# Pair products with batch norm: rows of a pair matrix stored from two permanent slots, a long row beside a short one

## The chip, the core and the metric

The kernel runs on one core of a Trainium2 chip. A core has five engines that work beside each other: TensorE (PE in the profile), VectorE (DVE), ScalarE (ACT), GpSimd (POOL) and SyncE (SP), which here only issues transfers. Data come from HBM into SBUF (128 partitions) and go back by 16 DMA engines. The metric is the device time of one execution in microseconds (us); the median of three runs before the change is 2237.81 us (2237.63 to 2238.28).

## The reference

```python
B, F0, F1, E, C = (256, 39, 39, 16, 1)        # the inputs have 1024 samples
_ROWS, _COLS = np.tril_indices(F1, k=-1)      # 741 pairs (r, c) with c < r
cross = xj[:, rows, :, None] * xi[:, cols, None, :]
mean = jnp.mean(cross, axis=(0, 2, 3), keepdims=True)
var = jnp.mean(jnp.square(cross - mean), axis=(0, 2, 3), keepdims=True)
normed = (cross - mean) * jax.lax.rsqrt(var + BN_EPS)
normed = normed * gamma[None, :, None, None] + beta[None, :, None, None]
out = normed[:, :, None, :, :] * W[None, None, :, :, :]
return jnp.transpose(out, (0, 2, 1, 3, 4))
```

For each of 1024 samples and 741 pairs (r, c) the 16 x 16 outer product of row r of `xj` and row c of `xi` is normalised with the pair's mean and variance over all samples and multiplied by `W`. All is float32. The inputs are 2.6 MB each; the output, 1024 x 741 x 256 numbers, is 777 MB.

## The kernel before, in words

**Layout.** Each of the 128 partitions holds 8 samples (`NT` = 8). A pair of one sample is 256 numbers, 1 KB; this is called a unit here. In the output the pairs of a row r lie side by side, so that r pairs of one sample are one run of r KB.

**Statistics.** The first part of the kernel computes, for each pair, a scale s and a shift t from sums over the samples; they end in `st_sb`, two numbers for each of the 741 pairs, the same on every partition. The last step of it (lines 216 to 234) goes through groups of rows, `ROW_GROUPS`: VectorE spreads a group on a diagonal (L219), TensorE multiplies it with ones (L226), and ScalarE copies each row of the group from PSUM to its place in `st_sb` (L234, 38 copies in all). Then ScalarE copies `W` into PSUM for VectorE (`w_dve`).

**Tiles.** The main part goes through tiles. A tile is one row r (all r pairs with c < r) for `nt` of a partition's 8 samples. `samples(r)` takes the largest of 1, 2, 4, 8 with nt x r at most `UNITS` = 76: eight samples up to row 9, four for rows 10 to 19, two from row 20 on. The order of rows is 6, 7, ..., 38, then 5, 4, ..., 1; that makes 105 tiles. The buffers `y` (up to 76 units) and `xs` have two copies each.

**The three steps of a tile k.**
- `scale_xi(k)` (L256, GpSimd): xs = s times `xi`, one instruction.
- `products(k)`: y = xs times one number of `xj`. Above row 6, for each sample and each i of 16, one instruction over r x 16 numbers: ScalarE does 12 values of i (L282), GpSimd 4 (L284). In rows 1 to 6 VectorE does a whole sample in one instruction (L272).
- `finish(k)`: (y + t) times W. Of the pairs above row 6 some 13% (from `split` on) are GpSimd's: one L313 for each pair, adding t, then one L317 for all of them, multiplying by W. The other pairs are VectorE's, one L297 each, over all nt samples. SyncE stores `16 // nt` pairs at a time as VectorE gets them done (runs of 2, 4 or 8 KB), and GpSimd's pairs in a store of their own at the end (L307).

**Order.** All is written out by hand under `manual_schedule`, and each engine works in the order of the program: finish(k), products(k+1), scale_xi(k+2). Waits between engines follow from what is read and written: products wait for xs and until the buffer's stores have landed, finish waits for the products, a store for its pairs. SyncE issues the stores in their order, and a store that has to wait holds up those behind it.

Of the kernel before, what the change touches and what calls it, by code (L numbers as in the profile page):

```python
# [7 lines left out]
F32 = mybir.dt.float32  # L8
AF = mybir.ActivationFunctionType
ALU = mybir.AluOpType  # L10
# [3 lines left out]

VECTOR_ROW = 6

UNITS = 76

POOL_I = 4
POOL_SHARE = 0.13  # L20

DEV_ON_VECTOR = ((2, 1), (4, 1), (6, 1))

ROW_GROUPS = ((1, 7), (7, 13), (13, 19), (19, 25), (25, 31), (31, 37), (37, 39))


@with_exitstack
def tile_pair_outer_batchnorm(
# [15 lines left out]
    nc = tc.nc  # L44
    P = nc.NUM_PARTITIONS
    NB, F, E = xi.shape
    NT = NB // P
    EE = E * E
# [4 lines left out]
    xi_sb = cpool.tile([P, NT, F, E], F32, name="xi_sb")  # L53
    xj_sb = cpool.tile([P, NT, F, E], F32, name="xj_sb")
    w_sb = cpool.tile([P, 1, EE], F32, name="w_sb")
    st_sb = cpool.tile([P, 2, NP], F32, name="st_sb")
    s_sb = st_sb[:, 0:1].unsqueeze(3)
    t_sb = st_sb[:, 1]
# [3 lines left out]
    out_v = out.rearrange("(p t) o n i j -> p t (o n i j)", t=NT)  # L62
# [6 lines left out]
    with tc.tile_pool(name="stat", bufs=1) as st, tc.tile_pool(  # L69
        name="dev", bufs=3  # L70
    ) as devp, tc.tile_pool(name="ps", bufs=1, space=bass.MemoryType.PSUM) as psp, tc.tile_pool(
        name="psx", bufs=3, space=bass.MemoryType.PSUM
# [6 lines left out]
        for r in range(1, F):  # L79
            n0 = first[r]  # L80
# [99 lines left out]
        u, v = shift_r, shift[0:F, 1, :]  # L180
        stt = nc.vector.scalar_tensor_tensor

        def small(name):
            return st.tile([F, F], F32, name=name)

        k, q1, q2, var, rstd, inv = (small(n) for n in ("k", "q1", "q2", "var", "rstd", "inv"))
# [28 lines left out]

        for r0, r1 in ROW_GROUPS:
            n = r1 - r0
# [19 lines left out]
    w_dve = wpsp.tile([P, 1, EE], F32, name="w_dve")  # L237
# [1 line left out]

    def samples(r):
        return max(n for n in (1, 2, 4, 8) if NT % n == 0 and (n == 1 or n * r <= UNITS))

    order = list(range(VECTOR_ROW, F)) + list(range(VECTOR_ROW - 1, 0, -1))
    tiles = [(r, t0, samples(r)) for r in order for t0 in range(0, NT, samples(r))]

    rows = ctx.enter_context(tc.tile_pool(name="rows", bufs=2))
    scaled = ctx.enter_context(tc.tile_pool(name="scaled", bufs=2))
    xs_of, y_of = {}, {}  # L250

    def scale_xi(k):
        r, t0, nt = tiles[k]
        n0 = first[r]
        xs = scaled.tile([P, nt, r, E], F32, tag="xs", name=f"xs_{r}_{t0}")
        nc.gpsimd.tensor_tensor(  # L256
            xs,
            xi_sb[:, t0 : t0 + nt, 0:r, :],
            s_sb[:, :, n0 : n0 + r, :].to_broadcast([P, nt, r, E]),
            ALU.mult,  # L260
        )
        xs_of[k] = xs

    def products(k):

        r, t0, nt = tiles[k]
        xs = xs_of.pop(k)
        y = rows.tile([P, nt, r, E, E], F32, tag="y", name=f"y_{r}_{t0}")
        y_of[k] = y
        for t in range(nt):  # L270
            if r <= VECTOR_ROW:
                nc.vector.tensor_tensor(  # L272
                    y[:, t],
                    xs[:, t].unsqueeze(2).to_broadcast([P, r, E, E]),
                    xj_sb[:, t0 + t, r : r + 1, :].unsqueeze(3).to_broadcast([P, r, E, E]),
                    ALU.mult,
                )
                continue
            for i in range(E):
                scale = xj_sb[:, t0 + t, r, i : i + 1]  # L280
                if i < E - POOL_I:
                    nc.scalar.activation(y[:, t, :, i, :], xs[:, t], AF.Copy, scale=scale)  # L282
                else:
                    nc.gpsimd.tensor_scalar(  # L284
                        y[:, t, :, i, :], xs[:, t], scale, 1.0, ALU.mult, ALU.mult
                    )

    def finish(k):

        r, t0, nt = tiles[k]  # L290
        n0 = first[r]
        y = y_of.pop(k).rearrange("p t n i j -> p t n (i j)")
        split = r - (int(r * POOL_SHARE + 0.5) if r > VECTOR_ROW else 0)
        step = max(1, 16 // nt)

        def pair(c):
            nc.vector.scalar_tensor_tensor(  # L297
                y[:, :, c, :],
                y[:, :, c, :],
                t_sb[:, n0 + c : n0 + c + 1],  # L300
                w_dve.to_broadcast([P, nt, EE]),
                ALU.add,
                ALU.mult,
            )

        def store(c0, c1):
            nc.sync.dma_start(  # L307
                out_v[:, t0 : t0 + nt, (n0 + c0) * EE : (n0 + c1) * EE],
                y[:, :, c0:c1, :].rearrange("p t n e -> p t (n e)"),
            )  # L310

        for c in range(split, r):
            nc.gpsimd.tensor_scalar(  # L313
                y[:, :, c, :], y[:, :, c, :], t_sb[:, n0 + c : n0 + c + 1], 1.0, ALU.add, ALU.mult
            )
        if split < r:
            nc.gpsimd.tensor_tensor(  # L317
                y[:, :, split:r, :],
                y[:, :, split:r, :],
                w_sb.unsqueeze(1).to_broadcast([P, nt, r - split, EE]),  # L320
                ALU.mult,
            )
        for c0 in range(0, split, step):
            c1 = min(c0 + step, split)
            for c in range(c0, c1):
                pair(c)
            store(c0, c1)
        if split < r:
            store(split, r)

    with tc.manual_schedule():
        scale_xi(0)
        products(0)
        scale_xi(1)
        for k in range(len(tiles)):
            finish(k)
            if k + 1 < len(tiles):
                products(k + 1)
            if k + 2 < len(tiles):
                scale_xi(k + 2)  # L340


# [26 lines left out]
```

## Time and profile before

| what | value |
|---|---|
| median of three runs | 2237.81 us |
| the profiled execution's own time | 2239.29 us |
| span of its trace | 2237.6 us |
| VectorE busy | 1758.6 us (79%) |
| ScalarE busy | 1523.6 us (68%) |
| GpSimd busy | 1428.4 us (64%) |
| TensorE busy | 18.7 us (1%) |
| stores' queue (q1), share of 16 engines | 86.8% |
| HBM written | 776.99 MB |
| mean rate over the span | 350 GB/s |

How to read the profile: the page gives each engine's busy time, then the span in 40 equal slices, where a digit is the busy share of a slice in tenths (9 is 90% or more) and the DMA row is the mean share of the 16 DMA engines. A stretch is the same for a time span that one chooses. A group is all instructions of one line and shape: busy time, the mean duration of one in ns, and after the bar the idle time of the engine ahead of them, with what ended it. A row in order of time gives start, duration, engine, line, and how many instructions it merges (x24); in brackets stands the idle time ahead of it and what ended it. "issue" means that the profile shows nothing that was waited for. L297 is line 297 of the kernel.

### The profile page before, as it was taken

To read this page: it belongs to the slowest core of one execution; us is meant where nothing else is said; L and a number is where in the kernel's file an instruction comes from. 1 tells how busy PE (TensorE), PEld (TensorE's weight loads), DVE (VectorE), ACT (ScalarE), POOL (GpSimd) and SP (SyncE) were. 2 spreads that over 40 slices of the span, in tenths; PEclk is the share of its full clock that TensorE was granted. 3 is DMA by queue.
4 is the path that set the end of the run, shared out by engine and by line. 5 is a ranking of instruction groups with operands and counts; after the bars stand their busy time and mean duration, and the time that the engine had idled before them with its cause. 6 is when DMAs were issued, how large, how long until landed. Compare 5 with 4: busy or idle time off the path is not lost. (4 is left out here: it accounts for less than half of the span.)

```text
span 2237.6 us, 9393 instructions
## 1 busy us (share of the span) xinstructions
PE 18.7 (1%) x70; PEld 11.9 (1%) x70; DVE 1758.6 (79%) x2314; ACT 1523.6 (68%) x3127; POOL 1428.4 (64%) x1572
## 2 busy tenths in 40 slices
PE   1200000000000000000000000000000000000000
PEld 1100000000000000000000000000000000000000
DVE  6836656677776777878887888888889888888998
ACT  2697888888856676676767667667667677676620
POOL 2655677676556766666677766766757676776730
PEclk9555555555555555555555555555555555555555
DMA  2377888889998888989898999999999999999987
GB/s 94 116 271 275 313 330 340 326 346 365 370 359 347 348 337 347 368 345 377 361 383 364 385 374 390 381 380 395 394 400 386 396 400 403 402 404 405 404 350 265
DMA packets 171696, 782.86 MB, mean 350 GB/s; under 512 B 7752, under 2 KB 23112, under 8 KB 119400
## 3 DMA queue, kind: packets, MB, share of 16 engines
q1 hardware_dynamic: 170924, 779.58, 86.8%
q10 hardware_dynamic: 652, 2.56, 0.3%
q14 instruction: 72, 0.59, 0.1%
q0 software_dynamic: 48, 0.13, 0.1%
HBM read 5.25 MB, written 776.99 MB: 350 GB/s over the span
## 5 line engine op out<-in xcount | busy, mean ns | idle before, releaser
L297 DVE SCALAR_TENSOR_TENSOR y<-y,st_sb,w_dve 128x512 f32<-128x512 f32 (+2 forms) x2208 | 1665.5, 835 | 442.4 <-issue 410.4
L282 ACT ACTIVATE y<-xs,xj_sb 128x112 f32<-128x112 f32 (+31 forms) x3072 | 1505.4, 586 | 559.4 <-DMA out_dram<-y 349.6
L313 POOL TENSOR_SCALAR y<-y,st_sb 128x512 f32<-128x512 f32 (+2 forms) x331 | 243.0, 752 | 599.6 <-ACT y L282 599.6
L284 POOL TENSOR_SCALAR y<-xs,xj_sb 128x112 f32<-128x112 f32 (+31 forms) x1024 | 569.9, 581 | 61.8 <-DMA out_dram<-y 55.7
L317 POOL TENSOR_TENSOR y<-y,w_sb 128x2048 f32<-128x2048 f32 (+3 forms) x99 | 425.7, 4300 | 8.3
L256 POOL TENSOR_TENSOR xs<-xi_sb,st_sb 128x768 f32<-128x768 f32 (+20 forms) x105 | 182.3, 1736 | 75.2 <-DVE y L272 58.1
L272 DVE TENSOR_TENSOR y<-xs,xj_sb 128x1536 f32<-128x1536 f32 (+5 forms) x48 | 48.8, 1092 | 3.4 <-PE ps L226 3.4
L133 POOL TENSOR_TENSOR dev<-xj_sb,shift 128x1248 f32<-128x1248 f32 x4 | 9.3, 2327 | 36.1 <-ACT shift_r L127 28.4
L124 ACT ACT_TABLE_LOAD x1 | 1.3, 1283 | 29.4 <-DMA b_sq<-in_L_rec_beta_dram 29.4
L140 ACT ACTIVATE dev<-dev 128x1248 f32<-128x1248 f32 x8 | 10.0, 1245 | 14.7 <-POOL dev L133 11.5
L107 DVE TENSOR_REDUCE total<-xj_sb 128x78 f32<-128x1248 f32 x4 | 5.8, 1455 | 8.0 <-DMA xj_sb<-in_r_xj_dram 8.0
L144 DVE SCALAR_TENSOR_TENSOR fa<-total,shift 128x78 f32<-128x78 f32 x4 | 3.1, 763 | 10.7 <-ACT shift_r L127 10.7
L234 ACT COPY st_sb<-ps 128x2 f32<-128x2 f32 (+37 forms) x38 | 4.2, 221 | 9.0 <-PE ps L226 9.0
L226 PE MATMUL ps<-wide,ones 39*128 39x468 f32 (+1 forms) x14 | 10.2, 921 | 5.7 <-DVE wide L219 5.7
L219 DVE TENSOR_TENSOR wide<-stq,eye 39x468 f32<-39x468 f32 (+1 forms) x7 | 5.3, 778 | 2.5 <-PE ps L226 2.3
L142 DVE TENSOR_REDUCE fb<-dev 128x78 f32<-128x1248 f32 x4 | 5.7, 1441 | 1.4 <-ACT dev L140 1.4
L142 DVE TENSOR_REDUCE fa<-dev 128x78 f32<-128x1248 f32 x4 | 5.8, 1441 | 1.0 <-ACT dev L140 1.0
L156 PE MATMUL ps_g<-fb,fa 128*39 128x79 f32 x32 | 5.9, 339 | 40.0 <-DVE fb L142 40.0
L107 DVE TENSOR_REDUCE total<-xi_sb 128x78 f32<-128x1248 f32 x4 | 5.8, 1444 | 0.0
L133 DVE TENSOR_TENSOR dev<-xi_sb,shift 128x1248 f32<-128x1248 f32 x3 | 5.2, 1773 | 0.0
L144 DVE SCALAR_TENSOR_TENSOR fb<-total,shift 128x78 f32<-128x78 f32 x4 | 5.2, 1289 | 0.0
L226 PEld LDWEIGHTS ps<-wide,ones 39*128 39x128 f32 x14 | 4.5, 329 | 11.3 <-DVE wide L219 6.4
(46 smaller groups left out, 25.4 us busy)
## 6 DMA issues: line engine op xcount, KB each, us to landing
out_dram<-y SPq DMA_DIRECT2D x279, 2048.0 KB
out_dram<-y SPq DMA_DIRECT2D x69, 1024.0 KB
out_dram<-y SPq DMA_DIRECT2D x24, 1280.0 KB
out_dram<-y SPq DMA_DIRECT2D x36, 768.0 KB
out_dram<-y SPq DMA_DIRECT2D x16, 1536.0 KB
out_dram<-y SPq DMA_DIRECT2D x12, 1792.0 KB
out_dram<-y SPq DMA_DIRECT2D x18, 512.0 KB
out_dram<-y SPq DMA_DIRECT2D x12, 256.0 KB
```

The source lines that it names most:

```text
L107: nc.vector.tensor_reduce(total[:, t0 : t0 + TS, x], src[:, t0 : t0 + TS], AX.X, ALU.add)
L133: engine.tensor_tensor(dev, src[:, t0 : t0 + TS], shift[:, x : x + 1, :].unsqueeze(3).to_broadcast([P, TS, F, E]), ALU.subtract,)
L140: nc.scalar.activation(dev, dev, AF.Square, scale=0.25)
L142: nc.vector.tensor_reduce(to, dev, AX.X, ALU.add)
L226: nc.tensor.matmul(ps.rearrange("p r x f -> p (r x f)"), ones[0:F, :], wide.rearrange("p r f -> p (r f)"), start=True, stop=True,)
L256: nc.gpsimd.tensor_tensor(xs, xi_sb[:, t0 : t0 + nt, 0:r, :], s_sb[:, :, n0 : n0 + r, :].to_broadcast([P, nt, r, E]), ALU.mult,)
L272: nc.vector.tensor_tensor(y[:, t], xs[:, t].unsqueeze(2).to_broadcast([P, r, E, E]), xj_sb[:, t0 + t, r : r + 1, :].unsqueeze(3).to_broadc ...
L282: nc.scalar.activation(y[:, t, :, i, :], xs[:, t], AF.Copy, scale=scale)
L284: nc.gpsimd.tensor_scalar(y[:, t, :, i, :], xs[:, t], scale, 1.0, ALU.mult, ALU.mult)
L297: nc.vector.scalar_tensor_tensor(y[:, :, c, :], y[:, :, c, :], t_sb[:, n0 + c : n0 + c + 1], w_dve.to_broadcast([P, nt, EE]), ALU.add, ALU ...
L313: nc.gpsimd.tensor_scalar(y[:, :, c, :], y[:, :, c, :], t_sb[:, n0 + c : n0 + c + 1], 1.0, ALU.add, ALU.mult)
L317: nc.gpsimd.tensor_tensor(y[:, :, split:r, :], y[:, :, split:r, :], w_sb.unsqueeze(1).to_broadcast([P, nt, r - split, EE]), ALU.mult,)
```

## The change: two slots, pairs of rows, longer stores

All tiles have two samples (`T` = 2). One buffer `y_sb` of 2 x 76 units is allocated once and cut into two slots of 76 units. Row 19 comes first, two tiles in each slot. Then for r = 20, ..., 38 and each pair of samples a slot is filled with row r (2r units) and beside it row 38 - r (76 - 2r units); row 38 fills a slot alone. There are 152 tiles, in the order long, short, long, short.

A row is stored in equal pieces of up to 14 pairs (`PIECE`): one piece up to row 14, two up to row 28, three above, 288 stores in all instead of 466. GpSimd's pairs no longer have a store of their own; they go with the last pieces.

The order in the loop is now: products(k+1) if they are ScalarE's and GpSimd's (row above 6), scale_xi(k+2), finish(k), and then products(k+1) if they are VectorE's. So GpSimd has its part of products(k+1) and scale_xi(k+2) ahead of its part of finish(k). `ROW_GROUPS` has the same groups with that of rows 19 to 24 first.

```diff
-UNITS = 76
+T = 2
+PIECE = 14
-ROW_GROUPS = ((1, 7), (7, 13), (13, 19), (19, 25), (25, 31), (31, 37), (37, 39))
+ROW_GROUPS = ((19, 25), (13, 19), (25, 31), (7, 13), (31, 37), (1, 7), (37, 39))
...
-    def samples(r):
-        return max(n for n in (1, 2, 4, 8) if NT % n == 0 and (n == 1 or n * r <= UNITS))
-
-    order = list(range(VECTOR_ROW, F)) + list(range(VECTOR_ROW - 1, 0, -1))
-    tiles = [(r, t0, samples(r)) for r in order for t0 in range(0, NT, samples(r))]
-
-    rows = ctx.enter_context(tc.tile_pool(name="rows", bufs=2))
+    half = T * (F - 1)
+    tiles = []
+    slot = 0
+    mid = (F - 1) // 2
+    for t0 in range(0, NT, T):
+        tiles.append((mid, t0, slot * half + (t0 // T % 2) * half // 2))
+        slot ^= t0 // T % 2
+    for r in range(mid + 1, F):
+        for t0 in range(0, NT, T):
+            tiles.append((r, t0, slot * half))
+            if r < F - 1:
+                tiles.append((F - 1 - r, t0, slot * half + T * r))
+            slot ^= 1
+
+    rows = ctx.enter_context(tc.tile_pool(name="rows", bufs=1))
     scaled = ctx.enter_context(tc.tile_pool(name="scaled", bufs=2))
+    y_sb = rows.tile([P, 2 * half, EE], F32, name="y_sb")
...
-        y = rows.tile([P, nt, r, E, E], F32, tag="y", name=f"y_{r}_{t0}")
-        y_of[k] = y
-        for t in range(nt):
+        y = y_sb[:, u : u + T * r, :].rearrange("p (t n) (i j) -> p t n i j", t=T, i=E)
+        for t in range(T):
...
-        for c0 in range(0, split, step):
-            c1 = min(c0 + step, split)
-            for c in range(c0, c1):
-                pair(c)
-            store(c0, c1)
-        if split < r:
-            store(split, r)
+        pieces = -(-r // PIECE)
+        for q in range(pieces):
+            c0, c1 = q * r // pieces, (q + 1) * r // pieces
+            for c in range(c0, min(c1, split)):
+                nc.vector.scalar_tensor_tensor(
+                    y[:, :, c, :],
+                    y[:, :, c, :],
+                    t_sb[:, n0 + c : n0 + c + 1],
+                    w_dve.to_broadcast([P, T, EE]),
+                    ALU.add,
+                    ALU.mult,
+                )
+            nc.sync.dma_start(
+                out_v[:, t0 : t0 + T, (n0 + c0) * EE : (n0 + c1) * EE],
+                y[:, :, c0:c1, :].rearrange("p t n e -> p t (n e)"),
+            )
 
     with tc.manual_schedule():
         scale_xi(0)
         products(0)
         scale_xi(1)
         for k in range(len(tiles)):
-            finish(k)
-            if k + 1 < len(tiles):
+            if k + 1 < len(tiles) and tiles[k + 1][0] > VECTOR_ROW:
                 products(k + 1)
             if k + 2 < len(tiles):
                 scale_xi(k + 2)
+            finish(k)
+            if k + 1 in xs_of:
+                products(k + 1)
```

More of the change, by code (lines that the diff above doesn't have):

```diff
@@ L238, in tile_pair_outer_batchnorm @@
     nc.scalar.copy(w_dve, w_sb)
-    def samples(r):
-        return max(n for n in (1, 2, 4, 8) if NT % n == 0 and (n == 1 or n * r <= UNITS))
-    order = list(range(VECTOR_ROW, F)) + list(range(VECTOR_ROW - 1, 0, -1))
-    tiles = [(r, t0, samples(r)) for r in order for t0 in range(0, NT, samples(r))]
-    rows = ctx.enter_context(tc.tile_pool(name="rows", bufs=2))
+    half = T * (F - 1)
[12 more added lines that the diff above has]
+    rows = ctx.enter_context(tc.tile_pool(name="rows", bufs=1))
     scaled = ctx.enter_context(tc.tile_pool(name="scaled", bufs=2))
-    xs_of, y_of = {}, {}
+    y_sb = rows.tile([P, 2 * half, EE], F32, name="y_sb")
+    xs_of = {}
     def scale_xi(k):
-        r, t0, nt = tiles[k]
+        r, t0, _ = tiles[k]
         n0 = first[r]
-        xs = scaled.tile([P, nt, r, E], F32, tag="xs", name=f"xs_{r}_{t0}")
+        xs = scaled.tile([P, T, r, E], F32, tag="xs", name=f"xs_{r}_{t0}")
         nc.gpsimd.tensor_tensor(
             xs,
-            xi_sb[:, t0 : t0 + nt, 0:r, :],
-            s_sb[:, :, n0 : n0 + r, :].to_broadcast([P, nt, r, E]),
+            xi_sb[:, t0 : t0 + T, 0:r, :],
+            s_sb[:, :, n0 : n0 + r, :].to_broadcast([P, T, r, E]),
             ALU.mult,
@@ L264, in products @@
     def products(k):
-        r, t0, nt = tiles[k]
+        r, t0, u = tiles[k]
         xs = xs_of.pop(k)
-        y = rows.tile([P, nt, r, E, E], F32, tag="y", name=f"y_{r}_{t0}")
-        y_of[k] = y
-        for t in range(nt):
+        y = y_sb[:, u : u + T * r, :].rearrange("p (t n) (i j) -> p t n i j", t=T, i=E)
+        for t in range(T):
             if r <= VECTOR_ROW:
@@ L288, in finish @@
     def finish(k):
-        r, t0, nt = tiles[k]
+        r, t0, u = tiles[k]
         n0 = first[r]
-        y = y_of.pop(k).rearrange("p t n i j -> p t n (i j)")
+        y = y_sb[:, u : u + T * r, :].rearrange("p (t n) e -> p t n e", t=T)
         split = r - (int(r * POOL_SHARE + 0.5) if r > VECTOR_ROW else 0)
[L294 to L310, printed above, removed]
         for c in range(split, r):
@@ L319, in finish @@
                 y[:, :, split:r, :],
-                w_sb.unsqueeze(1).to_broadcast([P, nt, r - split, EE]),
+                w_sb.unsqueeze(1).to_broadcast([P, T, r - split, EE]),
                 ALU.mult,
             )
-        for c0 in range(0, split, step):
-            c1 = min(c0 + step, split)
-            for c in range(c0, c1):
-                pair(c)
-            store(c0, c1)
-        if split < r:
-            store(split, r)
+        pieces = -(-r // PIECE)
[14 more added lines that the diff above has]
+            )
     with tc.manual_schedule():
```

## The prediction

> **What bounds the kernel now.** I read the page first (slices, DMA queues), then the stretches, then the groups with their forms, then the order of time in the last long rows and at the start. The slices and the queue of the stores:
>
> ```profile
> span 2237.6 us, 9393 instructions
> PE 18.7 (1%) x70; PEld 11.9 (1%) x70; DVE 1758.6 (79%) x2314; ACT 1523.6 (68%) x3127; POOL 1428.4 (64%) x1572
> DVE  6836656677776777878887888888889888888998
> DMA  2377888889998888989898999999999999999987
> GB/s 94 116 271 275 313 330 340 326 346 365 370 359 347 348 337 347 368 345 377 361 383 364 385 374 390 381 380 395 394 400 386 396 400 403 402 404 405 404 350 265
> DMA packets 171696, 782.86 MB, mean 350 GB/s; under 512 B 7752, under 2 KB 23112, under 8 KB 119400
> q1 hardware_dynamic: 170924, 779.58, 86.8%
> ```
>
> The output is 1024 x 741 KB = 777.0 MB. The stores' queue keeps 16 engines busy for 86.8% of 2237.6 = 1942 us, so about 295 us of transfer time is lost: at the start, in stretches where the DMA row shows 7 to 9, and in the last two slices. Only toward the end do its GB/s pass 400, and no compute engine is above 79% over the span. Four stretches show why even the busy time is not one price (columns: length, busy us of PE, PEld, DVE, ACT, POOL, clock, DMA share, GB/s):
>
> ```profile
> 112.00:185.00 73.00, 0.00 (x0) 0.00 (x0) 35.05 (x16) 72.86 (x240) 46.38 (x87) 0.50 0.72 261
> 340.00:420.00 80.00, 0.00 (x0) 0.00 (x0) 52.17 (x45) 68.93 (x181) 56.62 (x77) 0.50 0.87 340
> 690.00:820.00 130.00, 0.00 (x0) 0.00 (x0) 96.84 (x146) 91.73 (x193) 88.42 (x104) 0.50 0.85 341
> 2050.00:2120.00 70.00, 0.00 (x0) 0.00 (x0) 61.08 (x93) 50.25 (x72) 47.85 (x46) 0.50 0.99 407
> ```
>
> Dividing GB/s by share gives the rate of a fully busy queue: 362, 391, 401, 411. The runs stored there, counted from the loops, have a mean of 1.7 KB (rows 7 to 9), 3.2 KB (rows 13 to 16), 5.3 KB (rows 21, 22) and 6.3 KB (row 38: 8, 8, 8, 8, 1 and 5 KB). Counted over all rows, before stores 162,816 runs, 52,224 of them of 8 KB; the page has 171,696 - 119,400 = 52,296 packets of 8 KB or more, so one run is one packet. From the first and last stretch a packet costs 12.4 ns + 0.0370 ns per byte of one engine (16 x 1741 / 362.5 = 76.8 ns; 16 x 6485 / 411.1 = 252.4 ns); for 3.2 KB that gives 392 GB/s, where 391 is read.
>
> The last long row in order of time shows the wait that closes the loop:
>
> ```profile
> 2067.35 21.82 DVE L297 SCALAR_TENSOR_TENSOR y<-y,st_sb,w_dve 128x512 f32<-128x512 f32 x33 [3.76 <-issue]
> 2074.70 16.75 ACT L282 ACTIVATE y<-xs,xj_sb 128x608 f32<-128x608 f32 x24 [7.44 <-DMA out_dram<-y]
> 2076.45 6.02 POOL L284 TENSOR_SCALAR y<-xs,xj_sb 128x608 f32<-128x608 f32 x8
> 2082.43 2.28 POOL L256 TENSOR_TENSOR xs<-xi_sb,st_sb 128x1216 f32<-128x1216 f32 x1
> 2091.54 21.81 DVE L297 SCALAR_TENSOR_TENSOR y<-y,st_sb,w_dve 128x512 f32<-128x512 f32 x33 [2.37 <-issue]
> 2091.62 3.37 POOL L313 TENSOR_SCALAR y<-y,st_sb 128x512 f32<-128x512 f32 x5 [6.92 <-ACT y L282]
> 2095.07 5.59 POOL L317 TENSOR_TENSOR y<-y,w_sb 128x2560 f32<-128x2560 f32 x1
> 2099.30 16.75 ACT L282 ACTIVATE y<-xs,xj_sb 128x608 f32<-128x608 f32 x24 [7.85 <-DMA out_dram<-y]
> 2123.43 0.80 ACT L282 ACTIVATE y<-xs,xj_sb 128x608 f32<-128x608 f32 x1 [7.38 <-issue]
> ```
>
> ScalarE refills a buffer only when all its stores have landed; products take 16.8 us, VectorE's first 8 pairs 8 x 0.661 = 5.3 us, then the stores: 2091.54 + 5.29 = 2096.83 to 2123.43 is 26.6 us, of which 9.96 MB at 411 GB/s is 24.2, so 2.4 us are latency. Together 48.7 us for two tiles, 24.4 each: here the loop just fills the DMA. A 40-unit tile (row 20) uses half of the same buffer, with the same loop of products, pairs and latency against half the transfer; so DMA idles there.
>
> **The change part by part.** The groups that carry the costs (busy us, mean ns; the mean counts overlap with the next one twice, so I use busy / count):
>
> ```profile
> L282 ACT ACTIVATE y<-xs,xj_sb 128x592 f32<-128x592 f32 x96 | 65.7, 779 | 30.3 <-DMA out_dram<-y 14.9 <-POOL y L317 9.2 <-DVE y L297 6.2
> L282 ACT ACTIVATE y<-xs,xj_sb 128x496 f32<-128x496 f32 x96 | 58.0, 697 | 25.9 <-DMA out_dram<-y 11.8 <-POOL y L317 7.6 <-DVE y L297 6.5
> L282 ACT ACTIVATE y<-xs,xj_sb 128x320 f32<-128x320 f32 x96 | 44.0, 550 | 32.0 <-DMA out_dram<-y 32.0
> L282 ACT ACTIVATE y<-xs,xj_sb 128x304 f32<-128x304 f32 x96 | 42.5, 537 | 10.1 <-DMA out_dram<-y 10.1
> L282 ACT ACTIVATE y<-xs,xj_sb 128x288 f32<-128x288 f32 x96 | 41.2, 523 | 9.7 <-DMA out_dram<-y 9.7
> L297 DVE SCALAR_TENSOR_TENSOR y<-y,st_sb,w_dve 128x512 f32<-128x512 f32 x1912 | 1265.6, 744 | 260.5 <-issue 247.3 <-ACT y L282 13.2
> L297 DVE SCALAR_TENSOR_TENSOR y<-y,st_sb,w_dve 128x1024 f32<-128x1024 f32 x254 | 304.5, 1277 | 143.7 <-issue 125.2 <-ACT y L282 18.5
> L297 DVE SCALAR_TENSOR_TENSOR y<-y,st_sb,w_dve 128x2048 f32<-128x2048 f32 x42 | 95.6, 2344 | 38.2 <-issue 38.0
> L272 DVE TENSOR_TENSOR y<-xs,xj_sb 128x1536 f32<-128x1536 f32 x8 | 13.7, 1779 | 3.4 <-PE ps L226 3.4
> L272 DVE TENSOR_TENSOR y<-xs,xj_sb 128x1280 f32<-128x1280 f32 x8 | 11.3, 1487 | 0.0
> L272 DVE TENSOR_TENSOR y<-xs,xj_sb 128x1024 f32<-128x1024 f32 x8 | 9.2, 1221 | 0.0
> L284 POOL TENSOR_SCALAR y<-xs,xj_sb 128x320 f32<-128x320 f32 x32 | 16.4, 534 | 11.8 <-DMA out_dram<-y 10.4 <-issue 1.4
> L317 POOL TENSOR_TENSOR y<-y,w_sb 128x1536 f32<-128x1536 f32 x28 | 96.2, 3435 | 2.3
> ```
>
> *Slots.* A slot of 76 units is now always filled, row r beside row 38-r: 78 fills of 9.96 MB instead of tiles of 40 to 76 units. For the DMA to stay busy, a region must be refilled in the time in which the other regions drain. Row 20: products 24 x 0.458 (44.0 us / 96) = 11.0 us, first piece of 10 pairs 6.6, latency 2.4, own drain 12.7: 32.7 us of the 48 that two fills take. Row 31 (form 128x496): 58.0 / 4 = 14.5, with 6.6 + 2.4 + 19.7 that is 43.2. The engines' work in a fill must also be below some 24 us. ScalarE's instructions are the same ones, 24 per row and tile: rows 20 and 18 together (44.0 + 41.2) / 4 = 21.3 us. *Tiles of two samples* cost VectorE: 254 instructions of 1024 become 508 of 512, 42 of 2048 become 168, at 1265.6 / 1912 = 0.662 us: 676 x 0.662 - 304.5 - 95.6 = +47 us, to 2588 pairs or 1713 us, with the short products (L272, same 48) some 1760 us. In a fill that is 33 x 0.661 = 21.8 us. Both hide under the DMA, with 2.3 us to spare; without that cover the 47 us would show. GpSimd gets 45 more L313 and 47 more L256 (under 25 us, even at 0.5 each), beside 809 us of idle time. The short products stay behind finish(k) on VectorE, as before.
>
> *Rows 32 to 34* break the cover: 34 pairs (22.5 us) and short products of 2 x 1.71, 1.41 or 1.15 us make VectorE's fill 25.9, 25.3 and 24.8 us against 24.1 (below). Over four fills each that is 15 us, less the 3 or so that is stored up in finished tiles: 12 us.
>
> *Longer stores.* Runs of up to 14 KB: 73,728 packets, mean 10.5 KB, and 288 issues for 466. By the fit the stores' time goes from (162,816 x 12.4 + 777.0e6 x 0.0370) / 16 = 1924 us to 1855 us. The two-decimal shares allow 9 to 16 ns a packet, which saves 50 to 89 us, which gives 1835 to 1874. No row shows a run above 8 KB; the nearest, the 411 GB/s stretch, is what I extend. At a share of 0.985, between the 0.99 of that stretch and the 0.98 that the slices of 402 to 405 GB/s make of 411, 1855 becomes 1883 us, 24.1 a fill. The Trainium skill ("DMA: Bandwidth & Descriptors", section Bandwidth) puts a packet at about 10.5 ns, from loads of another queue; by it the saving is 58 us and the sum below 10 us longer, and the 12.4 ns of these stretches is near it.
>
> The longer first piece costs loop time in the longest rows, where hardly anything else lies in the slot. Twelve pairs take 7.9 us, not 5.3. Row 38: 16.8 + 7.9 + 2.4 + 24.1 = 51.2 for two fills, 25.6 each; row 37, with 16.4 of products and 23.5 of drain, 50.2, so 25.1; row 36, by the same steps, 49.2, so 24.6; row 35 (first piece 11 pairs) 47.7, hidden. Four fills each: 2 + 4 us for rows 36 and 37.
>
> *Products ahead of finish on GpSimd.* GpSimd now issues products(k+1), which wait for a region to drain, and scale_xi(k+2) ahead of its own pairs of tile k. These pairs now go out in the last piece with VectorE's, not in a store of their own, so that piece waits on SyncE, with every later store behind it. Rows 20 to 31: that region was filled four tiles ago, a whole fill is still queued behind it, and GpSimd's chain (row 20: 8 x 0.51 for L284, some 1.2 for an xs at the rate of the 2.28 above, 3 x 0.67 and 3.4 for its pairs, 11 us) fits. Rows 32 to 37: the tile next to a long row is a short one of VectorE, so nothing is put ahead but an xs. Row 38: k+1 takes the slot of k-1, and after its landing come 6.0 + 2.3 + 3.4 + 5.6 = 17.3 us on GpSimd, then 13 of 38 pairs to store, 8.2, and 2.4 latency: 27.9 us. Two fills at 27.9, one at 25.6, the last free: 9 us.
>
> *Start and end.* Before, the first store leaves at 93.54:
>
> ```profile
> 67.21 3.59 POOL L256 TENSOR_TENSOR xs<-xi_sb,st_sb 128x768 f32<-128x768 f32 x2 [17.02 <-ACT st_sb L234]
> 68.19 0.57 ACT L234 COPY st_sb<-ps 128x14 f32<-128x14 f32 x6 [1.05 <-PE ps L226]
> 75.32 18.85 ACT L282 ACTIVATE y<-xs,xj_sb 128x112 f32<-128x112 f32 x67
> 93.54 0.64 SPq L307 DMA_DIRECT2D out_dram<-y  x1
> ```
>
> ScalarE still has to do all 38 copies before it starts at 75.3, so the new group order only brings xs of row 19 early, which is hidden. Then 24 x 0.443 = 10.6 us of products and 9 pairs, 6.0: first store at 92. From there half slots of row 19 come every 11.2 us (17 pairs), a half drains in 12. At the end the short rows are gone from the tail:
>
> ```profile
> 2228.99 2.35 DVE L297 SCALAR_TENSOR_TENSOR y<-y,st_sb,w_dve 128x2048 f32<-128x2048 f32 x1
> ```
>
> From its end (2231.3) the span goes on 6.3 us, of which a 1 MB store takes 2.6; about 4 us stay.
>
> Sum: 92 + 1883 + 12 + 6 + 9 + 4 = 2006 us. The profiled execution took 2239.29 us for its span of 2237.6, the median of the runs is 2237.81, so span and median are the same to 0.2: 2006.
>
> **The rivals.** *Runs over 8 KB are cut.* Pieces of 9 to 14 pairs, 60,416 of the packets, then count twice: (134,144 x 12.4 + 777.0e6 x 0.0370) / 16 / 0.985 = 1930 us, and the sum is 2053. For: nothing above 8 KB is in the trace. Against: one run was one packet at every size.
>
> *VectorE is the bound.* It has 152 tiles, and in the rows above it idles 2.4 to 3.8 us ahead of one. Its work from 86 us (first products done) is 1760; with 1.5 us of idle time a tile it ends at 86 + 1760 + 228 + 14 (last piece and end) = 2088. Against: those idle gaps stand in a stretch at 0.99 of DMA, where they cost nothing, and a region is now ready earlier.
>
> *Slower: GpSimd's loop of row 38 in every fill.* If the stores and products of one tile y_sb were ordered as a whole slot and not by region, each fill would wait as row 38 does: 92 + 78 x 27.9 + 4 = 2272. It decides from 27.5 us a fill ((2238 - 96) / 78). Against: st_sb is one tile too, and its xs began at 67.21 while copies into other rows of it began at 68.19, so overlap is followed by region. Beside it stands a rule: the Trainium skill ("SBUF — State Buffer", section Summary: rules for kernel authors) counts about 358 GB/s for any transfer to or from HBM. By it 777 MB take 2170 us and the sum is 2293, slower too; the trace disagrees, with 407 GB/s over 70 us.
>
> **How the numbers follow.** The forecast 0.72, with its own range 1960 (packets dear, 1835 / 0.99, half the 27 us of bubbles) to 2045 (packets cheap, 1874 / 0.98, and 10 us more of bubbles, with gaps in the ramp); cut runs 0.10; VectorE's idle time 0.11; slower 0.05; no change 0.02, if idle time per tile reaches 2.5 us. The range reaches over the forecast and the first rivals: 1960 to 2090. Under 0.2%, or 4.5 us, this kernel's runs tell nothing. Faster 0.93, same 0.02, slower 0.05.
>
> **What would show it.** Right: the DMA row at 9 from the third slice to the last but one, 400 to 418 GB/s; about 82,000 packets; VectorE near 1806 us busy, 90%; the first store near 92 us; fills of 24 us in rows 20 to 31, 26 in row 32, about 28 in row 38. Wrong: packets near 140,000 (cut runs); DMA at 8 in the middle with VectorE's wait on ScalarE's products (second rival); GpSimd's L284 waiting on stores with SyncE waiting on L317 in every row (third). The forecast falls if full queues move less than 405 GB/s with the long runs.

## The result, and the profile after

The changed kernel takes 1979.56 us (median of 4 runs, 1979.46 to 1979.84), the kernel before 2237.86 us beside it: a ratio of 0.8846, 95% interval 0.883 to 0.8861. That is 258 us less. The forecast was 2006 us.

The page of the profiled execution after the change, in the order in which the prediction read the one before (span, busy time, slices, packets, the stores' queue):

```profile
span 1977.9 us, 9219 instructions
PE 18.6 (1%) x70; PEld 11.8 (1%) x70; DVE 1802.4 (91%) x2694; ACT 1519.2 (77%) x3127; POOL 1437.4 (73%) x1693
DVE  5599999999998999999999999999999999999886
DMA  2199999999999999999999999999999999999998
GB/s 106 47 421 421 420 421 421 421 421 421 422 425 425 423 425 425 425 423 425 424 421 422 420 421 418 412 389 386 393 392 403 403 411 411 407 407 403 395 379 375
DMA packets 79760, 782.84 MB, mean 396 GB/s; under 512 B 4905, under 2 KB 5929, under 8 KB 14153
q1 hardware_dynamic: 78988, 779.57, 94.3%
```

In the changed kernel L267 is `scale_xi`; L282 are VectorE's products, L292 ScalarE's and L294 GpSimd's; L305 and L309 finish GpSimd's pairs, L319 VectorE's; L327 issues the stores.

The DMA row stands at 9 from the third slice to the last but one. The stores' queue is busy for 94.3% of 1977.9 = 1865 us, against 1942 before: 77 us less busy time, from fewer and longer runs. The idle rest fell from 295 to 113 us, and most of that lies ahead of the first store, which leaves at 92.60. So 182 of the span's 260 us come from transfers that no longer wait. VectorE does 44 us more work than before and is busy for 91% of a shorter span.

The packets can be counted to the last. The queue's 78,988 are 73,728 runs, 16 for each of the 288 stores, and 652 of its loads (the other queue of loads, q10, has as many). The kernel before has 162,816 + 16 x 466 + 652 = 170,924, as its page says. So a run of up to 14 KB is one packet, and every store adds 16.

The GB/s row falls into three parts: 418 to 425 from the third to the 25th slice, a dip to 386, and a tail that sinks from 411 to 375. The same in stretches (length, busy us of PE, PEld, DVE, ACT, POOL, clock, DMA share, GB/s): rows 19 to 30, then the dip.

```profile
105.00:1195.00 1090.00, 0.00 (x0) 0.00 (x0) 1008.11 (x1527) 981.80 (x2218) 894.73 (x1152) 0.50 1.01 422
1251.00:1551.00 300.00, 0.00 (x0) 0.00 (x0) 297.74 (x426) 181.53 (x288) 182.01 (x183) 0.50 0.95 396
```

In the first the DMA is full (a share of 1.01, where full is 1) and no other engine is. In the second VectorE is busy 297.7 of 300 us and the DMA is not full: the bound has changed hands. VectorE's rows in order of time, in row 32, show it:

```profile
1284.68 3.42 DVE L282 TENSOR_TENSOR y_sb<-xs,xj_sb 128x1536 f32<-128x1536 f32 x2
1288.13 22.48 DVE L319 SCALAR_TENSOR_TENSOR y_sb<-y_sb,st_sb,w_dve 128x512 f32<-128x512 f32 x34
1310.52 3.42 DVE L282 TENSOR_TENSOR y_sb<-xs,xj_sb 128x1536 f32<-128x1536 f32 x2
```

No row has a bracket, so there is no idle time: 3.4 us of short products and 34 pairs repeat every 25.8 us. ScalarE's rows give the length of every fill (from the start of one long row to the start of the next), since it starts a long row when that region's stores have landed. These are the first fills of rows 29, 32, 33, 34, 35, 36 and 37, then the four of row 38:

```profile
964.20 21.17 ACT L292 ACTIVATE y_sb<-xs,xj_sb 128x464 f32<-128x464 f32 x48 [1.99 <-DMA out_dram<-y_sb]
1251.35 14.80 ACT L292 ACTIVATE y_sb<-xs,xj_sb 128x512 f32<-128x512 f32 x24 [2.19 <-DMA out_dram<-y_sb]
1347.96 15.12 ACT L292 ACTIVATE y_sb<-xs,xj_sb 128x528 f32<-128x528 f32 x24 [9.90 <-DMA out_dram<-y_sb]
1450.03 15.45 ACT L292 ACTIVATE y_sb<-xs,xj_sb 128x544 f32<-128x544 f32 x24 [9.24 <-DMA out_dram<-y_sb]
1551.43 15.77 ACT L292 ACTIVATE y_sb<-xs,xj_sb 128x560 f32<-128x560 f32 x24 [9.58 <-DMA out_dram<-y_sb]
1650.05 16.09 ACT L292 ACTIVATE y_sb<-xs,xj_sb 128x576 f32<-128x576 f32 x24 [8.63 <-DMA out_dram<-y_sb]
1747.63 16.42 ACT L292 ACTIVATE y_sb<-xs,xj_sb 128x592 f32<-128x592 f32 x24 [7.72 <-DMA out_dram<-y_sb]
1847.41 16.73 ACT L292 ACTIVATE y_sb<-xs,xj_sb 128x608 f32<-128x608 f32 x24 [8.38 <-DMA out_dram<-y_sb]
1872.03 16.73 ACT L292 ACTIVATE y_sb<-xs,xj_sb 128x608 f32<-128x608 f32 x24 [7.89 <-DMA out_dram<-y_sb]
1898.95 16.73 ACT L292 ACTIVATE y_sb<-xs,xj_sb 128x608 f32<-128x608 f32 x24 [10.18 <-DMA out_dram<-y_sb]
1925.87 16.73 ACT L292 ACTIVATE y_sb<-xs,xj_sb 128x608 f32<-128x608 f32 x24 [10.20 <-DMA out_dram<-y_sb]
```

Differences over the number of fills: rows 29 to 31 take 23.9 us a fill (287.15 / 12), row 32 24.2, row 33 25.5, row 34 25.4, row 35 24.7, row 36 24.4, row 37 24.9, and row 38 24.6, 26.9, 26.9.

### The profile page after: what moved, and what is told of

Same layout as the page of the kernel before. It is cut to its first block, busy times and chain, and to the rows that moved or that the text cites. A ratio compares the mean times of both kernels' runs of the same rounds, so it can differ in the third digit from the quotient of the medians.

```text
span 1977.9 us, 9219 instructions
## 1 busy us (share of the span) xinstructions
PE 18.6 (1%) x70; PEld 11.8 (1%) x70; DVE 1802.4 (91%) x2694; ACT 1519.2 (77%) x3127; POOL 1437.4 (73%) x1693
## 2 busy tenths in 40 slices
DMA packets 79760, 782.84 MB, mean 396 GB/s; under 512 B 4905, under 2 KB 5929, under 8 KB 14153
## 3 DMA queue, kind: packets, MB, share of 16 engines
q1 hardware_dynamic: 78988, 779.57, 94.3%
## 5 line engine op out<-in xcount | busy, mean ns | idle before, releaser
L319 DVE SCALAR_TENSOR_TENSOR y_sb<-y_sb,st_sb,w_dve 128x512 f32<-128x512 f32 x2588 | 1711.0, 742 | 133.5 <-issue 96.7
L292 ACT ACTIVATE y_sb<-xs,xj_sb 128x320 f32<-128x320 f32 (+21 forms) x3072 | 1500.8, 581 | 366.2 <-DMA out_dram<-y_sb 324.6
L294 POOL TENSOR_SCALAR y_sb<-xs,xj_sb 128x320 f32<-128x320 f32 (+22 forms) x1024 | 556.7, 566 | 188.9 <-DMA out_dram<-y_sb 155.3
L309 POOL TENSOR_TENSOR y_sb<-y_sb,w_sb 128x1024 f32<-128x1024 f32 (+4 forms) x128 | 431.2, 3369 | 10.7
L267 POOL TENSOR_TENSOR xs<-xi_sb,st_sb 128x608 f32<-128x608 f32 (+37 forms) x152 | 190.0, 1253 | 275.5 <-DVE y_sb L282 178.5
L305 POOL TENSOR_SCALAR y_sb<-y_sb,st_sb 128x512 f32<-128x512 f32 x376 | 253.8, 692 | 1.7 <-ACT y_sb L292 1.7
L282 DVE TENSOR_TENSOR y_sb<-xs,xj_sb 128x1536 f32<-128x1536 f32 (+5 forms) x48 | 50.1, 1085 | 0.0
L236 ACT COPY st_sb<-ps 128x38 f32<-128x38 f32 (+37 forms) x38 | 4.3, 219 | 8.7 <-PE ps L228 8.7
L158 PEld LDWEIGHTS ps_g<-fb,fa 128*39 128x39 f32 x32 | 4.3, 182 | 42.0 <-issue 30.9
(46 smaller groups left out, 25.3 us busy)
```

What stands on the lines that cost most here:

```text
L158: nc.tensor.matmul(acc[0:F, 0 : 2 * F + 1], lhs, fb[:, t], start=t == 0, stop=t == NT - 1)
L267: nc.gpsimd.tensor_tensor(xs, xi_sb[:, t0 : t0 + T, 0:r, :], s_sb[:, :, n0 : n0 + r, :].to_broadcast([P, T, r, E]), ALU.mult,)
L282: nc.vector.tensor_tensor(y[:, t], xs[:, t].unsqueeze(2).to_broadcast([P, r, E, E]), xj_sb[:, t0 + t, r : r + 1, :].unsqueeze(3).to_broadc ...
L294: nc.gpsimd.tensor_scalar(y[:, t, :, i, :], xs[:, t], scale, 1.0, ALU.mult, ALU.mult)
L305: nc.gpsimd.tensor_scalar(y[:, :, c, :], y[:, :, c, :], t_sb[:, n0 + c : n0 + c + 1], 1.0, ALU.add, ALU.mult)
L309: nc.gpsimd.tensor_tensor(y[:, :, split:r, :], y[:, :, split:r, :], w_sb.unsqueeze(1).to_broadcast([P, T, r - split, EE]), ALU.mult,)
```

## The experiments

The theory after the result: the slots keep the DMA full, and that is most of the gain; the longer runs give a small part; what is left comes from VectorE in rows 32 to 34 and from the loop of the longest rows. The rivals: the longer stores carry the gain; two-sample tiles in the new order suffice; GpSimd's new order matters. All times below are medians beside runs of the kernel before, with the 95% interval of the ratio to it.

### The slots with the short stores

```diff
-        pieces = -(-r // PIECE)
...
+        for c0 in range(0, split, 8):
+            c1 = min(c0 + 8, split)
...
+            store(c0, c1)
+        if split < r:
+            store(split, r)
```

> The changed kernel with the stores of before: 8 pairs at a time and GpSimd's pairs in a store of their own (520 stores, 133,120 packets instead of 73,728). Theory (the slots carry the gain, the longer runs a small part): rows 19 to 31 stay bound by the DMA and pay 12.4 ns a packet, 0.69 us a fill or 35 us over 50 fills; rows 32 to 35 are bound by VectorE and pay nothing; rows 36 to 38 get some 10 us back from a first piece of 8 pairs: about 2005 us, DMA share still 1.0 in rows 20 to 31. Rival (the longer stores carry the gain, the slots little): 2150 us or more.

Measured: 1998.41 us, ratio 0.893 (0.8917 to 0.8943). All of the change but the stores (slots, two-sample tiles, order) keeps 239 of the 258 us. The page's GB/s row and queue, and the stretch over rows 19 to 30:

```profile
GB/s 105 58 408 412 410 411 412 412 412 411 412 411 411 410 412 412 411 412 411 411 411 411 411 411 410 411 406 390 391 392 399 402 408 413 415 414 415 408 409 392
q1 hardware_dynamic: 142092, 779.59, 96.1%
105.00:1195.00 1090.00, 0.00 (x0) 0.00 (x0) 984.76 (x1492) 955.53 (x2161) 874.62 (x1123) 0.50 1.02 411
```

The DMA is as full as with long stores, only slower: a fill of 9.962 MB takes 24.24 us at 411 GB/s and 23.61 at 422. By the loops a fill of rows 20 to 30 has 1792 packets here and 908 there on average; 0.63 us x 16 engines / 884 is 11.4 ns a packet. The prediction's fit had 12.4. The queue is busy for 96.1% of 1996.7 = 1919 us: of the 77 us less busy time 23 come with the two-sample tiles and 54 with the longer pieces. Only 19 of these 54 reach the time. At the start of row 32 this kernel is 31 us behind the changed one (1282.39 against 1251.35), and by the end it has won 12 back, 7 of them in row 38 and the end, where a shorter first piece was expected to help.

### The long stores without the slots

```diff
-        for c0 in range(0, split, step):
-            c1 = min(c0 + step, split)
-            for c in range(c0, c1):
+        pieces = -(-r // 14)
+        for q in range(pieces):
+            c0, c1 = q * r // pieces, (q + 1) * r // pieces
+            for c in range(c0, min(c1, split)):
                 pair(c)
             store(c0, c1)
-        if split < r:
-            store(split, r)
```

> The kernel before with nothing changed but the stores: whole rows or equal pieces of up to 14 pairs, GpSimd's pairs in them. Theory (without the slots the wait for the buffer closes the loop, and a longer first piece lengthens it): some 0.8 us more for each two-sample tile, about 3 for the four-sample and 7 for the eight-sample tiles, less packet time notwithstanding: slower than before, about 2340 us, with the packets down to about 55,000 to 80,000. Rival (packet cost was the bound): 1942 us of DMA time shrink by 70, about 2170 us.

Measured: 2362.46 us, ratio 1.0557 (1.054 to 1.0575): the same stores that save 19 us with the slots cost 125 without them. Its slices, its queue and ScalarE's wait for the stores, and then that wait in the kernel before (us in all, times, longest):

```profile
DMA  2257566778887887787888888989989998999986
q1 hardware_dynamic: 78076, 779.57, 78.9%
ACT y L282 <- DMA out_dram<-y: 665.6, 93, 18.7
```

```profile
ACT y L282 <- DMA out_dram<-y: 349.6, 62, 16.6
```

The queue's busy time did fall, from 1942 to 78.9% of 2360.6 = 1863 us, just as with the slots. But the queue waits longer: VectorE must finish up to 14 pairs before the first store of a tile can leave, and ScalarE waits for the buffer's stores for 666 us in all, where it was 350.

### The same tiles without shared slots

The tiles, their order and the stores are the changed kernel's, but each tile gets one of two buffers in turn, so that all long rows go through one of them and all short rows through the other.

```diff
-    rows = ctx.enter_context(tc.tile_pool(name="rows", bufs=1))
+    rows = ctx.enter_context(tc.tile_pool(name="rows", bufs=2))
-    y_sb = rows.tile([P, 2 * half, EE], F32, name="y_sb")
...
-        y = y_sb[:, u : u + T * r, :].rearrange("p (t n) (i j) -> p t n i j", t=T, i=E)
+        y = rows.tile([P, T, r, E, E], F32, tag="y", name=f"y_{r}_{t0}")
```

> The changed kernel with the same tiles, order and stores, but each tile in a buffer of its own, two buffers of 76 units in turn, so that long rows share one buffer and short rows the other: the release of a region is put back to the release of the tile before the last. Theory (the loop of products, first piece, own drain and latency sets a fill where only the short partner drains beside it): 32 us a fill in row 20, 43 in row 31, 50 in row 37: about 3240 us. Rival (two-sample tiles in this order with long stores suffice, the shared slots are not needed): below 2150 us.

Measured in a single run, without an interval: 3252.93 us. ScalarE's first two fills of rows 31 and 37 in order of time:

```profile
1828.87 21.19 ACT L292 ACTIVATE y<-xs,xj_sb 128x496 f32<-128x496 f32 x48 [19.95 <-DMA out_dram<-y]
1871.24 21.16 ACT L292 ACTIVATE y<-xs,xj_sb 128x496 f32<-128x496 f32 x48 [21.18 <-DMA out_dram<-y]
2923.74 16.39 ACT L292 ACTIVATE y<-xs,xj_sb 128x592 f32<-128x592 f32 x24 [32.40 <-DMA out_dram<-y]
2973.11 16.40 ACT L292 ACTIVATE y<-xs,xj_sb 128x592 f32<-128x592 f32 x24 [32.97 <-DMA out_dram<-y]
```

A fill takes 42.4 us in row 31 and 49.4 in row 37, the loop of products, first piece, own drain and latency; the brackets show half to two thirds of it as the wait for the stores. With the shared slots the same loop is just as long, but it runs over two fills, because a whole other slot drains meanwhile. The run shows what this overlap is worth in the new order of tiles; other plans of buffers were not tried.

### Finish ahead of products on GpSimd

```diff
-            if k + 1 < len(tiles) and tiles[k + 1][0] > VECTOR_ROW:
+            finish(k)
+            if k + 1 < len(tiles):
                 products(k + 1)
             if k + 2 < len(tiles):
                 scale_xi(k + 2)
-            finish(k)
-            if k + 1 in xs_of:
-                products(k + 1)
```

> The changed kernel with the loop order of before: finish(k), products(k+1), scale_xi(k+2). Theory (the DMA is the bound in rows 20 to 31, so that GpSimd's order is slack there, and only row 38 is held up by it, 26.9 us a fill instead of 25.6): 3 to 5 us faster, about 1975 us, row 38 at 25.6. Rival (the new order is needed, since GpSimd's part of a short tile's products would come after 7 to 9 us of finish and hold up VectorE by about 3 us in rows 24 to 31): DMA share below 0.97 there and 2000 to 2080 us.

Measured: 2055.73 us, ratio 0.9186 (0.9172 to 0.92), 76 us slower than the changed kernel. The theory that the order is slack fell. The rival's time came true, and so did its share (0.92 over rows 29 to 31), but not its reason. The first line of its waits (us in all, times, longest), and one fill of row 30 in order of time:

```profile
ACT y_sb L292 <- POOL xs L267: 373.3, 57, 11.5
```

```profile
1098.71 2.70 POOL L305 TENSOR_SCALAR y_sb<-y_sb,st_sb 128x512 f32<-128x512 f32 x4 [6.62 <-ACT y_sb L292]
1101.49 4.52 POOL L309 TENSOR_TENSOR y_sb<-y_sb,w_sb 128x2048 f32<-128x2048 f32 x1
1106.00 2.81 POOL L294 TENSOR_SCALAR y_sb<-xs,xj_sb 128x128 f32<-128x128 f32 x8
1108.76 1.84 POOL L267 TENSOR_TENSOR xs<-xi_sb,st_sb 128x960 f32<-128x960 f32 x1
1110.63 21.18 ACT L292 ACTIVATE y_sb<-xs,xj_sb 128x480 f32<-128x480 f32 x48 [5.08 <-POOL xs L267]
```

ScalarE waits for the xs of the next long row, not VectorE for GpSimd's products. When the long row's products end, GpSimd does 7.2 us of finish, 2.8 of products and 1.8 of xs; ScalarE's short tile is done sooner and stands for 5.1 us. In the changed kernel the xs is ahead of finish. The same wait stands ahead of ScalarE's long rows up to row 37, where it is 11.4 us. (The fill of row 30 is 26.25 us: 1110.63 to the next such row at 1136.88.)

### Only the xs ahead of finish

```diff
-            if k + 1 < len(tiles) and tiles[k + 1][0] > VECTOR_ROW:
-                products(k + 1)
             if k + 2 < len(tiles):
                 scale_xi(k + 2)
             finish(k)
-            if k + 1 in xs_of:
+            if k + 1 < len(tiles):
                 products(k + 1)
```

> The changed kernel with the order scale_xi(k+2), finish(k), products(k+1): GpSimd has only the xs ahead of its pairs, and its products(k+1) behind them again. Theory (in finish-first ScalarE waited for the xs that stood behind finish and products on GpSimd, and not for GpSimd's own products): rows 20 to 31 are bound by the DMA again, 23.9 us a fill, and row 38 loses the loop over GpSimd's products, 25.6 us a fill instead of 26.9: 1975 us, 2 to 6 below the changed kernel. Rival (GpSimd's products have to come ahead of finish): 2020 us or more.

Measured: 2051.52 us, ratio 0.9167 (0.9154 to 0.9179). Half of the theory held: up to row 31 the GB/s are those of the changed kernel, 419 to 426. From row 32 on they fall to about 350, for a reason that it did not have, and row 38, expected at 25.6 us a fill, takes 28.9, 30.5 and 23.8. Two of its waits, then a fill of row 35:

```profile
POOL xs L267 <- DVE y_sb L282: 279.1, 24, 12.8
...
DVE y_sb L319 <- POOL y_sb L294: 90.3, 24, 7.6
```

```profile
1650.05 1.82 DVE L282 TENSOR_TENSOR y_sb<-xs,xj_sb 128x768 f32<-128x768 f32 x2
1651.91 2.06 DVE L319 SCALAR_TENSOR_TENSOR y_sb<-y_sb,st_sb,w_dve 128x512 f32<-128x512 f32 x3
1651.95 0.35 POOL L267 TENSOR_TENSOR xs<-xi_sb,st_sb 128x96 f32<-128x96 f32 x1 [10.47 <-DVE y_sb L282]
1652.28 5.68 POOL L294 TENSOR_SCALAR y_sb<-xs,xj_sb 128x560 f32<-128x560 f32 x8
1657.99 19.84 DVE L319 SCALAR_TENSOR_TENSOR y_sb<-y_sb,st_sb,w_dve 128x512 f32<-128x512 f32 x30 [4.02 <-POOL y_sb L294]
```

The 0.35 us of xs for the next short row must wait until VectorE's short products (L282) have read the xs buffer that it takes (10.5 us of idle time). Behind it on GpSimd stand the 8 products of the long row, and behind these waits VectorE. A fill takes 28 us in rows 33 to 37, where the changed kernel takes 24.4 to 25.5. In the changed kernel these products go ahead of that xs; the same wait (178.5 us in all) holds up none of them there.

### VectorE's short products moved

```diff
-VECTOR_ROW = 6
+VECTOR_ROW = 3
```

> The changed kernel with VECTOR_ROW 3: the products of rows 4 to 6 go to ScalarE and GpSimd, and one pair of each to GpSimd. Theory (rows 32 to 34 are bound by VectorE, 25.4 us a fill): VectorE falls to 21.8 us a fill there, ScalarE rises from 15 to 21, the fills take the DMA's 23.7: about 25 us faster, 1955 us, GB/s above 415 in those rows. Rival (the rate falls there because of the short partner rows' small runs): unchanged within 3 us, GB/s still 388 to 406.

Measured: 1963.98 us, ratio 0.8776 (0.8763 to 0.8789), 15.6 us less than the changed kernel. The same rows 32 to 34 in a stretch:

```profile
1251.00:1538.00 287.00, 0.00 (x0) 0.00 (x0) 261.39 (x397) 254.13 (x576) 233.11 (x301) 0.50 1.00 415
```

VectorE is free for 26 of 287 us, the DMA is full, and the 12 fills take 287 us, not 300. The cause is shown; the expected 25 us were too much. The dip of the changed kernel takes 25.0 us a fill, not 25.4, because the first fills lived on finished tiles, and a fill here takes 23.9 us, not 23.7, with the DMA at 415 GB/s.

### Shorter pieces in the longest rows

```diff
-        pieces = -(-r // PIECE)
+        pieces = -(-r // (PIECE if r < 35 else 10))
```

> The changed kernel with pieces of at most 10 pairs from row 35 on and nothing else. Theory (loop of the longest rows: 2 to 3 pairs less in the first piece, 1.3 to 2.0 us in two fills; in row 38 the last piece 2 us shorter): row 37 at 24.2 us a fill, row 38 at 25.9: 8 us less, about 1971 us. Rival (these rows are bound by VectorE's backlog or the DMA's rate): within 2 us of 1979.6.

Measured: 1968.14 us, ratio 0.8794 (0.8782 to 0.8806), 11.4 us less. Row 37 runs from its first start to that of row 38:

```profile
1744.80 16.41 ACT L292 ACTIVATE y_sb<-xs,xj_sb 128x592 f32<-128x592 f32 x24 [7.87 <-DMA out_dram<-y_sb]
1842.09 16.73 ACT L292 ACTIVATE y_sb<-xs,xj_sb 128x608 f32<-128x608 f32 x24 [8.33 <-DMA out_dram<-y_sb]
```

That is 24.3 us a fill, from 24.9: the first piece is part of the loop there. Row 37 gives some 2.5 of the 11.4 us, rows 35 and 36 some 2.8, and row 38 with the end of the kernel 5.9 (124.6 us from its first start, where it was 130.5).

### All three

This kernel joins the three edits above.

```diff
-VECTOR_ROW = 6
+VECTOR_ROW = 3
...
+        pieces = -(-r // (PIECE if r < 35 else 10))
...
+            if k + 2 < len(tiles):
+                scale_xi(k + 2)
+            finish(k)
+            if k + 1 < len(tiles):
+                products(k + 1)
```

> The order of xs-first, VECTOR_ROW 3, and pieces of at most 10 pairs from row 35 on (9 or 10 pairs instead of 11 to 13). Theory (in the longest rows the loop of products, first piece, latency and own drain is the bound; 3 pairs less in the first piece are 2.0 us in two fills): row 36 hidden, row 37 at 24.1 us a fill, row 38 at 24.6: 12 to 14 us below the run with VECTOR_ROW 3, about 1951 us. Rival (packets or the DMA's rate set the fills of the longest rows): 1961 us or more, rows 36 to 38 as in the run with VECTOR_ROW 3.

Measured: 1999.38 us, ratio 0.8934 (0.8922 to 0.8946), slower than the changed kernel. Its row 37, again to the start of row 38:

```profile
1751.77 16.41 ACT L292 ACTIVATE y_sb<-xs,xj_sb 128x592 f32<-128x592 f32 x24 [11.32 <-DMA out_dram<-y_sb]
1864.22 16.73 ACT L292 ACTIVATE y_sb<-xs,xj_sb 128x608 f32<-128x608 f32 x24 [11.71 <-DMA out_dram<-y_sb]
```

That is 28.1 us a fill. In rows 35 to 37 (25.3, 28.0 and 28.1 us a fill) the order of xs-first still meets VectorE's short products, those of rows 3 to 1. Two kernels were to tell whether the order as such is at fault. The first keeps the moved products and the short pieces, and goes back to the changed kernel's order except in row 38:

```diff
-            if k + 1 < len(tiles) and tiles[k + 1][0] > VECTOR_ROW:
+            if k + 1 < len(tiles) and VECTOR_ROW < tiles[k + 1][0] and tiles[k][0] < F - 1:
```

> VECTOR_ROW 3, pieces of at most 10 pairs from row 35 on, and the changed kernel's order (products(k+1), scale_xi(k+2), finish(k)) but for row 38, which has scale_xi(k+2), finish(k), products(k+1). Theory (in xs-first the xs of the next short row, which waits for VectorE's short products, stood ahead of GpSimd's part of the next long row's products, and VectorE waited for these; in the changed kernel's order it stands behind them): rows 35 to 37 at 24 us a fill and not 28, row 38 at 24.6: 1952 us. Rival (finer pieces in the long rows slow the fills there): 1964 us or more.

The second keeps the order of xs-first and the short pieces and takes all products from VectorE:

```diff
-VECTOR_ROW = 6
+VECTOR_ROW = 0
```

> The order of xs-first, with VECTOR_ROW 0 (no products on VectorE at all) and pieces of at most 10 pairs from row 35 on. Theory (the order of xs-first costs 28 us a fill only where an xs waits for VectorE's short products): without these products the long rows take 24 to 24.6 us a fill with the same order: about 1952 us, no wait of GpSimd's xs for VectorE left. Rival (that order itself holds up the long rows): 28 us a fill in rows 35 to 37, 1990 us or more.

Measured: 1952.68 us, ratio 0.8725 (0.8713 to 0.8737), and 1952.71 us, ratio 0.8724 (0.8712 to 0.8736). In the first, rows 35 to 37 take 24.0, 24.1 and 24.2 us a fill. The one puts the xs back behind the products that VectorE needs, the other removes what the xs waited for. The longest wait of GpSimd in the second, and its row 37:

```profile
POOL xs L267 <- ACT y_sb L292: 308.6, 78, 6.6
```

```profile
1731.37 21.16 ACT L292 ACTIVATE y_sb<-xs,xj_sb 128x592 f32<-128x592 f32 x48 [2.60 <-DMA out_dram<-y_sb]
1827.75 16.73 ACT L292 ACTIVATE y_sb<-xs,xj_sb 128x608 f32<-128x608 f32 x24 [2.89 <-DMA out_dram<-y_sb]
```

No xs waits for VectorE any more, and a fill of row 37 takes 24.1 us, with the order that gave 28.1. Either is 27 us better than the changed kernel. By the sum, 15.6 us from the moved products and 11.4 from the shorter pieces account for the whole of it, and row 38's own order for nothing. The rows say otherwise. The last two starts of row 38 with the shorter pieces alone, then in the first of the two kernels:

```profile
1891.12 16.73 ACT L292 ACTIVATE y_sb<-xs,xj_sb 128x608 f32<-128x608 f32 x24 [9.06 <-DMA out_dram<-y_sb]
1916.26 16.73 ACT L292 ACTIVATE y_sb<-xs,xj_sb 128x608 f32<-128x608 f32 x24 [8.40 <-DMA out_dram<-y_sb]
```

```profile
1877.10 16.73 ACT L292 ACTIVATE y_sb<-xs,xj_sb 128x608 f32<-128x608 f32 x24 [9.07 <-DMA out_dram<-y_sb]
1900.73 16.73 ACT L292 ACTIVATE y_sb<-xs,xj_sb 128x608 f32<-128x608 f32 x24 [6.91 <-DMA out_dram<-y_sb]
```

The last fill takes 23.6 us instead of 25.1, after two that are alike (23.2 and 25.8 in both). So the order of row 38 gains 1.5 us. The sum hides it because both other edits shorten row 35 (from 24.7 us a fill to 23.9 and 24.1, and to 24.0 together), and that counts only once.

## Why the prediction was right, and where it was off

**The bound and its loop: right.** DMA that waits for refilled buffers was named as what the slots remove. The idle time of the stores' queue fell by 182 us; with the old stores 239 us of the gain remain; and the loop (products, first piece, drain, latency) gave fills of 43 and 50 us for the own buffers, measured 42.4 and 49.4.

**The DMA's term: mechanism right, size off.** This is the step that made the forecast too long, by 26 us in all. The fit of packets gave 1855 us of stores, and the whole queue, with its loads, measured 1865. But the prediction divided by a share of 0.985, taking the end of the trace before for a full queue. A full queue reads 1.01. At 422 GB/s a fill is 23.6 us and not 24.1; 78 fills are 1841 us, 42 less than the 1883 of the sum. The long runs were not cut: 79,760 packets, where about 82,000 were forecast.

**A ceiling at 358 GB/s: not there.** The rate that the page "SBUF — State Buffer" of the Trainium skill gives (section Summary: rules for kernel authors), about 358 GB/s, was no limit here: 422 GB/s held for 1090 us. The Trainium skill's page "HBM Reference" (section Specifications (TRN2)) says that a core streaming alone comes to about 425 GB/s, and with that the trace agrees.

**The bubbles: a little small.** Against 23.6 us a fill the span has about 1978 - 93 - 1841 - 4 = 40 us of them, where 27 were forecast against 24.1; this remainder also holds what the late rows lose by a rate below 422 GB/s. So two misses of opposite sign, 42 and 13 us, met in the forecast, and that it came so near is luck in that part. Most rows agree one by one: forecast and measured, row 33 25.3 and 25.5, row 34 24.8 and 25.4, row 36 24.6 and 24.4, row 37 25.1 and 24.9. Row 35 was to be hidden and took 24.7, since VectorE's backlog runs on into it (busy for 97.7 of the 99 us from 1551 to 1650). In row 32 tiles already finished covered the first fills: 25.9 was forecast, 24.2 measured.

**GpSimd's order: wrong in what it left out.** The prediction priced the new order at 9 us in row 38 and as slack elsewhere. Row 38's loop is there: 17.3 us from the landing at 1872.03 to the end of GpSimd's pairs at 1889.37, as forecast, and 9.6 instead of 10.6 for the last piece and its latency, so 26.9 us a fill and not 27.9. The prediction did not see that scale_xi(k+2), moved ahead of finish(k), is what keeps ScalarE fed: put back, this costs 76 us. Nor did it see that products ahead of the xs are right only because that xs can wait for VectorE. The sum came out all the same, because its argument for the order as it stands (GpSimd's chain fits) held, and the price of other orders does not enter it.

**The rest.** The first store left at 92.60 (92), where it was 93.54; the new order of `ROW_GROUPS` was not run by itself. VectorE's extra work was 44 us (47), hidden where the DMA is full and visible where it isn't. GpSimd's added instructions at 0.5 us each would be 46 us and not under 25, as the prediction has it; its busy time rose by 9, with no effect on the sum. Span and median lie 1.7 us apart in this kernel (1977.9 and 1979.56), not 0.2: the prediction set the span of one execution against the median of others. Of the rivals, cut runs are out by the packet count. VectorE as the bound is true of rows 32 to 34 and the backlog in row 35 alone. The third needed a region to wait for its whole slot; no such wait is seen, and the fills of 23.9 us leave no room for it.

## What to carry to other kernels

When transfers wait for buffers, write the loop of one buffer as a sum (refill, first piece, drain, latency) and ask what else can drain meanwhile; longer transfers alone can lengthen that sum, as they did here by 125 us. On an engine that works in order, a cheap instruction that feeds another engine belongs ahead of long work, but behind nothing that has to wait: 0.35 us in the wrong place cost about 3 us a fill in rows 33 to 37. Take the rate of a full queue from a stretch that is full, or by a fit at a share of 1, and not from the best stretch at hand.

## What was not expected of the hardware

A full queue of stores reads a share of 1.01 to 1.02 and moves 411 GB/s with runs of 5 to 6 KB on average and 420 to 425 with runs of 9 to 14 KB in the long rows. Each store adds 16 packets to those of its runs, in both kernels and also with the short stores (133,120 + 16 x 520 + 652 = 142,092). In rows 32 to 34, without VectorE's limit, the queue read 1.00 and moved 415 GB/s, some 5 less than the 420 of rows 29 to 31 with as many packets a fill, though a fill takes 23.9 us in both; why is open.
